# Twelve raw chunks gathered into the tiles of layer 0's weights and of the row vectors

## Chip, core and metric

One core of one Trainium2 chip. The metric is the device time of one launch in microseconds (us); the time of a kernel is the median of its runs. One further execution was recorded by the hardware profiler, and all rows quoted below are of that one. The engines are PE (matmuls), DVE (vector), ACT (scalar, activations), POOL (here the engine that issues gathers) and SP (here only the queue that issues plain transfers).

## What is computed

A graph with N = 6250 nodes of D = 512 features and E = 100000 edges, sorted by destination. Cut to what matters:

```
h = relu(layernorm(x))                         # no weights
norm[e] = -dinv[src[e]] * dinv[dst[e]]         # dinv = 1/sqrt(number of edges that leave a node), 0 for none
prop(h)[n] = sum over edges e into n of h[src[e]] * norm[e]
layer 1: h = leaky(layernorm(h @ W1_0 + prop(h) @ W1_1 + b1) * gamma + beta)   # slope 0.01
layer 2: out = h @ W2_0 + prop(h) @ W2_1 + b2
return x + out
```

All in fp32. The program calls the layers 0 and 1.

## The kernel before

**Stages.** A first stage loads x in 49 blocks of 128 rows, takes each block's mean and variance, makes relu(layernorm(x)), writes it into a table in HBM (`tab[0]`), and counts the edges that leave each node with one-hot matrices on DVE (L341) and matmuls. Then the two layers run one after the other, layer 0 reading `tab[0]` and writing `tab[1]`, layer 1 reading `tab[1]` and writing the output.

**Chunks and gathers.** The edges are cut into 782 chunks of 128. For each chunk POOL issues one indirect DMA that gathers 128 rows of a table, one for each edge, into a slot of the tile `places` (L237 in the first stage, L448 in the layers, L458 for the first 24 of layer 1). A row of `tab[0]` has 528 columns: 512 features, and behind them the node's dinv, so that DVE can scale the chunk's selection matrix by it (`scale`, L614).

**Raw chunks.** The first RAW = 64 chunks of layer 0 do not wait for the table. They are gathered from x itself as soon as the edges' sources are known, and made into relu(layernorm(x)) * dinv in place later: `find` (L481, matmuls that spread a chunk's indices, and a comparison on DVE) and `look_up` (L496, matmuls that fetch each edge's scale and bias; three DVE operations; then four activations, L507). One call of each does four chunks. They run three times a group of layer 0, until all raw chunks are done.

**Slots.** `places` has 63 slots. In the first stage the slots from 14 on hold the blocks of x; the 14 before them are free at once. Each block frees its slot when its write to the table has landed, and then a raw chunk may be gathered there (`make_table`, L306 to 315). The last eight slots later hold layer 1's weights (`w_late`), so the ring of gathers has R = 55 slots: chunk t goes to slot t modulo 55 and must wait until chunk t - 55 has been summed.

**Groups.** Three chunks make a unit, which covers 32 consecutive nodes; four units make a group (66 groups, g from 0; group g holds chunks 12g - 9 to 12g + 2). For a group DVE makes a 0/1 matrix (`choose`, L575), PE multiplies it with the gathered rows (`sums`, L627, 24 matmul passes), and ACT copies the result out (L637). When all groups that touch a block of 128 nodes are there, the block has its turn: `place` puts the groups' sums in the block's rows (L657), `first_half` transposes them and multiplies the block's own rows with W1_0 (`w_sb[1]`), `second` multiplies the sums with W1_1 (`w_sb[0]`), both at L536, and `finish` adds the bias and takes the layernorm (L718 to 740, with `bias1`, `gam`, `bet`).

**Order.** PE, POOL and SP run in the order in which the program is written; ACT and DVE are ordered by the scheduler. POOL's order is all gathers, one after the other. SP's order is in the first stage: loads of x, writes to the table, W1_1 after the first table write, four rows of 2 KB for the vectors, W1_0, the rest of the table, the dinv column of the first 31 blocks (L394); then loads of a block's own rows h two turns ahead (L513), and the blocks' results.

**Vectors.** `b1`, `b2`, `gamma` and `beta` are loaded as one row each (L205). After group 1 `widen` (L847 to 852) spreads each over 128 partitions by a matmul with a column of ones and a copy on DVE.

Of the kernel before, what the change touches and what calls it, by code (L numbers as in the profile page):

```python
# [9 lines left out]
F32 = mybir.dt.float32  # L10
# [3 lines left out]
OP = mybir.AluOpType  # L14
# [6 lines left out]
P = 128  # L21
# [4 lines left out]
Q = 32  # L26
NQ = P // Q
STEP = 3
DRIFT = 32
RE = 14  # L30
RAW = 64
PAD = 16
LATE = 3
AHEAD_OF = 24
# [9 lines left out]
def gnn_kernel(  # L44
# [33 lines left out]
    nc = tc.nc  # L78
    N, D = x.shape
# [5 lines left out]
    KD = D // P  # L85
    NC = -(-E // P)
# [4 lines left out]
    unit = [max(0, NU - NQ * (NS - g)) for g in range(NS + 1)]  # L91
# [16 lines left out]
    ident = const.tile([P, P], F32, name="ident")  # L108
# [13 lines left out]
    bias1 = const.tile([P, D], F32, name="bias1")  # L122
    bias2 = const.tile([P, D], F32, name="bias2")
    gam = const.tile([P, D], F32, name="gam")
    bet = const.tile([P, D], F32, name="bet")
    sidx = const.tile([P, NC], I32, name="sidx")
    eidx = const.tile([P, AHEAD_OF], I32, name="eidx")
    e_src = const.tile([P, AHEAD_OF, LATE], F32, name="e_src")
    w_sb = [const.tile([P, KD, D], F32, name=f"w{i}") for i in range(2)]
    sc = const.tile([P, 2, NB], F32, name="sc")  # L130
    pick = const.tile([P, P], BF, name="pick")
    src_lo = const.tile([P, P], BF, name="src_lo")
    src_hi = const.tile([P, RAW], F32, name="src_hi")
    p_id = const.tile([P, 1], F32, name="p_id")
# [4 lines left out]
    places = stay.enter_context(tc.tile_pool(name="places", bufs=1)).tile([P, RE + NB, W], F32, name="places")  # L139
    w_at = NB - 2 * KD  # L140
    R = RE + w_at
    w_late = places[:, R:, :D].rearrange("p (i k) d -> p i k d", i=2)

    nodes_ps = stay.enter_context(tc.tile_pool(name="nodes_ps", bufs=1, space=bass.MemoryType.PSUM)).tile(
        [P, D], F32, name="nodes_ps")
    assert NQ * NS + 1 <= D - P
# [15 lines left out]
    for ids, fill, name in ((src, 0, "src_c"), (dst, NO_NODE, "dst_c")):  # L162
        t = ep.tile([P, NG, P], I32, name=name)
# [17 lines left out]
    def load_x(i0, n):  # L181
        t = places[:, RE + i0 : RE + i0 + n, :D]
        full = sum(r == P for r in rows[i0 : i0 + n])
        if full:
            nc.sync.dma_start(t[:, :full, :],
                              x[i0 * P : (i0 + full) * P, :].rearrange("(i p) d -> p i d", p=P))
        for lo, hi in parts(rows[i0 + n - 1]) if full < n else ():
            at = (i0 + full) * P
            nc.sync.dma_start(t[lo:hi, full, :], x[at + lo : at + hi, :])
# [5 lines left out]
    def load_rest(k):  # L195
        if k < 3:
            load_x(*groups[6 + k])
        if k == 2:
            nc.sync.dma_start(tab[1][zero_row : zero_row + 1, :], places[P - 1 : P, RE + NB - 1, :D])
        if k == 3:  # L200
            for t, w in zip(w_sb, (W1_1, W1_0)):
                nc.sync.dma_start(t, w.rearrange("(k p) d -> p k d", p=P))
        if k == 1:
            for t, v in ((bias1, b1), (bias2, b2), (gam, gamma), (bet, beta)):
                nc.sync.dma_start(t[0:1], dup(v, 1))  # L205

    LO = P // 2
    HI = 2 * NB
# [15 lines left out]
    with tc.tile_pool(name="turn", bufs=1) as wp, tc.tile_pool(  # L224
        name="turn_ps", bufs=2, space=bass.MemoryType.PSUM
# [7 lines left out]
            nc.scalar.activation(sidx[:, g * P : g * P + n], fT[:, :n], AF.Copy)  # L233

    def gather_raw(lo, hi):
        for t in range(lo, min(hi, R)):
            nc.gpsimd.indirect_dma_start(  # L237
                out=places[:, t, :D], out_offset=None, in_=x,
                in_offset=bass.IndirectOffsetOnAxis(ap=sidx[:, t : t + 1], axis=0))

    gather_raw(0, RE)

    low = ep.tile([P, P], I32, name="low")
    nc.vector.tensor_single_scalar(low, chunks[0][:, 0, :], P - 1, op=OP.bitwise_and)
# [6 lines left out]
    with tc.tile_pool(name="turn", bufs=1) as wp, tc.tile_pool(  # L251
        name="turn_ps", bufs=1, space=bass.MemoryType.PSUM
# [23 lines left out]
        nc.vector.tensor_scalar_mul(minus, last, -1.0)  # L276
        high = ep.tile([P, RAW], I32, name="high")
        nc.vector.tensor_single_scalar(high, sidx[:, :RAW], 7, op=OP.arith_shift_right)
        nc.vector.tensor_copy(src_hi, high)
# [26 lines left out]
    def make_table(i0, n):  # L306

        for lo in range(i0, i0 + n, 2):
            hi = min(lo + 2, i0 + n)
            for i in range(lo, hi):  # L310
                v = places[:, RE + i, :D]
                nc.scalar.activation(v, v, AF.Relu, bias=nb_all[:, i : i + 1], scale=rs_all[:, i : i + 1])
            nc.sync.dma_start(tab[0][lo * P : hi * P, :].rearrange("(i p) d -> p i d", p=P),
                              places[:, RE + lo : RE + hi, :])
            gather_raw(RE + lo, RE + hi)

    some = [*groups[:6], (groups[6][0], NB - LAST - groups[6][0])]
    others = [(NB - LAST, groups[7][0] - (NB - LAST)), *groups[7:]]
# [6 lines left out]
    with tc.tile_pool(name="deg", bufs=1) as dp, tc.tile_pool(name="onehot", bufs=2) as ohp, tc.tile_pool(  # L325
        name="deg_ps", bufs=1, space=bass.MemoryType.PSUM
# [10 lines left out]
        for g in range(EJ // (2 * GJ)):  # L337
            hot = []
            for s, n, name in ((s_lo, LO, "lo"), (s_hi, HI, "hi")):
                t = ohp.tile([EP, GJ, n, 2], BF, name=name)  # L340
# [5 lines left out]
            k = turns.get(g)  # L346
# [15 lines left out]
    with tc.tile_pool(name="fold", bufs=1) as dp, tc.tile_pool(  # L362
        name="fold_ps", bufs=1, space=bass.MemoryType.PSUM
# [3 lines left out]
        for t in range(2):  # L367
            for i in range(2):
                nc.tensor.matmul(deg[t * LO : (t + 1) * LO, :], each[:, i, :], both[:, :, t, i],
                                 start=(i == 0), stop=(i == 1))  # L370
# [38 lines left out]
def usual_path(tc, have):  # L409
    nc = tc.nc  # L410
    (x, out, tab, h_tab, ndinv, sidx, dlx, iota_r, w_sb, W2_1, W2_0, w_late, ident, eps, ones, first, nodes_ps, node_of, minus,
     unsorted, dinv, sdinv, bias1, bias2, gam, bet, unseen, unit, N, E, D, NB, NC, NU, NS, KD, rows, places, R,
     load_rest, sc, pick, src_lo, src_hi, eidx, e_src, zero_row, p_id) = (
        have[n] for n in ("x out tab h_tab ndinv sidx dlx iota_r w_sb W2_1 W2_0 w_late ident eps ones first nodes_ps node_of "
                          "minus unsorted dinv sdinv bias1 bias2 gam bet unseen unit N E D NB NC NU NS KD rows places "
                          "R load_rest sc pick src_lo src_hi eidx e_src zero_row p_id").split())
    AHEAD = 2
    EARLY = {NB - 3: NS - 11, NB - 2: NS - 9, NB - 1: NS - 7}
    ACT = mybir.EngineType.Activation
# [8 lines left out]
    with ExitStack() as es:  # L428
        pool = es.enter_context(tc.tile_pool(name="main", bufs=2))
        psum = es.enter_context(tc.tile_pool(name="main_ps", bufs=2, space=bass.MemoryType.PSUM))  # L430
        es.enter_context(tc.manual_schedule(engines={PE, POOL, SP}))
        is_lo, found, looked, gathered = [], 0, 0, R
        behind, behind_rows, summed = {}, {}, {}
        own_h, own_x, agg, placed, started, pre, late, theres = {}, {}, {}, {}, {}, {}, {}, {}
        SHIFTED = D - D % P
# [3 lines left out]
        own_row, begun = {}, set()  # L439

        def zr(layer, t):
            return places[:, (layer * NC + t) % R, :D]

        def gather_to(layer, end):
            nonlocal gathered
            for t in range(gathered, min(end, NC)):
                own_scale = layer == 0 and t >= RAW
                nc.gpsimd.indirect_dma_start(  # L448
                    out=places[:, t % R, :] if own_scale else zr(layer, t), out_offset=None,
                    in_=x if layer == 0 and t < RAW else tab[layer],  # L450
                    in_offset=bass.IndirectOffsetOnAxis(
                        ap=lidx[:, t - SHIFTED : t - SHIFTED + 1] if layer and t >= SHIFTED else sidx[:, t : t + 1], axis=0))
            gathered = max(gathered, min(end, NC))
# [21 lines left out]
        def find(tag):  # L475
            nonlocal found
            if found == RAW:
                return
# [124 lines left out]
        def scale(sel, chunk, of=(0, NQ)):  # L603

            at = chunk[0][0]
            start = chunk[of[0]][0]
            end = chunk[min(of[1], len(chunk)) - 1][-1] + 1
            if end <= RAW:
                return
            each = sel.rearrange("p q s e -> p (q s) e")  # L610
            cut = sorted({start, end} | {t for t in range(start, end) if t % R == 0})
            for lo, hi in zip(cut, cut[1:]):
                v = each[:, lo - at : hi - at, :]
                last = nc.vector.tensor_tensor(  # L614
                    v, v, places[:, lo % R : lo % R + hi - lo, D : D + 1].to_broadcast([P, hi - lo, Q]), op=OP.mult)
            return last

        def sums(layer, g, sel, chunk, cnt=None, some=None, opens=True, closes=True):
# [65 lines left out]
        def end_block(layer):  # L684

            r = rows[END]
            aT = pool.tile([P, KD, P], F32, name="hT", bufs=1)
            nc.vector.tensor_copy(aT[:, :, :r], placed.pop(END)[:, :, :r])
            return aT
# [147 lines left out]

        find("ps")
        find("ps")
        load_rest(3)  # L840
        for i in range(AHEAD):
            load(0, i)
        for k in range(2):
            look_up("u_ps")
            find("ps")

        def widen():  # L847

            for t in (bias1, gam, bet, bias2):
                ps = psum.tile([P, D], F32, name="u_ps")  # L850
                nc.tensor.matmul(ps, ident[0:1, 0:1].to_broadcast([1, P]), t[0:1, :], start=True, stop=True)
                nc.vector.tensor_copy(t, ps)

        for layer in range(2):
            if layer == 1:
                gathered = AHEAD_OF
# [3 lines left out]
            for g in range(NS - 1):  # L860
# [44 lines left out]
                if layer == 0 and g == 13:  # L905
                    end_matrices()
                if layer == 0 and g == 1:
                    widen()
                if layer == 0 and g == NS - 16:
                    with tc.issue_after(scaled.ins):  # L910
                        shift(0, SHIFTED)
# [21 lines left out]
                if g == NS - 2:  # L933
# [30 lines left out]
                    end = end_block(layer)  # L964
# [333 lines left out]
```

## Time and profile before

| | |
|---|---|
| median of 3 runs | 2038.8 us (2034.94 to 2040.26) |
| profiled execution | 2041.34 us, its span 2039.4 us |
| mean granted clock of PE | 0.911 |
| busy: PE, POOL, DVE, ACT | 82%, 74%, 34%, 20% |
| moved by DMA | 527 MB, 259 GB/s over the span |
| first gather from the table | 132.83 us |
| layer 0 ends, first gather of layer 1 that needs all of its rows | 1066.69 us |
| last gather | 2016.58 us |

The profile's page gives busy times by engine, the span in 40 slices, the DMA queues, the chain of waits that ended last, and the costliest groups of instructions. A row of the timeline reads: start in us, duration in us, engine, line, operation, what it writes and reads, shape, count, and in brackets the engine's idle time before it with what ended it. A row of the view of windows reads: window, length, busy time of PE, PEld (weight loads), DVE, ACT and POOL with the number of their instructions, then the granted PE clock, the DMA share and GB/s. L numbers are lines of the kernel before.

### The profile page before, as it was taken

Reading aid. Unit: us, or ns where it says so; the run is one execution under the profiler, and the core shown is the slowest. Engines: PE = TensorE matmul, PEld = TensorE weight load, DVE = VectorE, ACT = ScalarE, POOL = GpSimd, SP = SyncE. Lnnn points to the kernel's source line nnn. Section 1 sums busy time; section 2 is a strip of 40 time slices with the busy share of each in tenths; the row PEclk is TensorE's granted clock in tenths of the full one; section 3 lists DMA queues with packets and bytes.
Section 4 is the critical chain, followed back from the end, with each engine's and each line's share of the span. In section 5 each row is a group of like instructions: output and inputs, shape, how many; then the busy total and the mean of one; then the engine's idle time right before and its main releaser. Section 6 shows DMA issues by size and latency. Waiting matters only on the chain.

```text
span 2039.4 us, 19969 instructions
## 1 busy us (share of the span) xinstructions
PE 1675.8 (82%) x6864; PEld 669.4 (33%) x6864; DVE 702.2 (34%) x1484; ACT 404.8 (20%) x738; POOL 1517.1 (74%) x1578
## 2 busy tenths in 40 slices
PE   5589987678797767887889888889888887988997
PEld 4454432223333222333333322223332332332333
DVE  7975543333453333443452221122121212121221
ACT  8784211111221111221210101001010010010110
POOL 5877777777777777777777777777777777777774
PEclk9789998889988888988999988899998899999999
DMA  9998888888888888888887888788788888888875
GB/s 350 377 310 256 274 263 253 255 240 263 282 277 253 253 258 246 262 268 252 247 258 238 247 251 251 240 257 252 240 256 248 247 249 256 247 246 251 274 237 161
DMA packets 189546, 527.46 MB, mean 259 GB/s; under 512 B 34576, under 2 KB 36350, under 8 KB 189436
## 3 DMA queue, kind: packets, MB, share of 16 engines
q0 software_dynamic: 125120, 415.98, 68.2%
q1 hardware_dynamic: 64316, 110.12, 15.1%
q8 instruction: 56, 0.92, 0.2%
q14 instruction: 54, 0.44, 0.1%
HBM read 474.31 MB, written 51.66 MB: 258 GB/s over the span
## 4 chain that ended last, share of the span: by engine, by line
PE 45%; DMA 23%; POOL 13%; issue 11%; DVE 6%; ACT 1%; DVEq 0%; POOLq 0%; ACTq 0%; SPq 0%
PE u_ps L536 18%; DMA places<-tab,sidx 16%; PE ps L627 14%; POOL places L448 13%; PE an_ps L657 8%; DMA places<-tab,lidx 6%; PE hT_ps L761 2%; PE hT_ps L524 2%; DVE hi L341 1%; DVE lo L341 1%; PE hT_ps L496 1%; DVE sel L614 1%; DVE st L721 0%; DMA places<-in_x_dram 0%; DVE u_ps L718 0%
## 5 line engine op out<-in xcount | busy, mean ns | idle before, releaser
L448 POOL DMA_INDIRECT places<-tab,sidx x1206 | 1147.3, 951 | 370.8 <-issue 272.2
L627 PE MATMUL ps<-places,sel 128*32 128x512 f32 x3128 | 521.2, 683 | 154.9 <-DMA places<-tab,sidx 84.1
L657 PE MATMUL an_ps<-agg,there 128*128 128x512 f32 (+1 forms) x572 | 279.8, 623 | 103.5 <-ACT agg L637 98.8
L448 POOL DMA_INDIRECT places<-tab,lidx x270 | 255.7, 947 | 82.3 <-issue 63.4
L627 PEld LDWEIGHTS ps<-places,sel 128*32 128x32 f32 x3128 | 104.5, 119 | 542.5 <-issue 200.8
L575 DVE TENSOR_TENSOR sel<-dlx,nodes_ps 128x384 f32<-128x384 f32 (+3 forms) x134 | 72.2, 540 | 416.4 <-PE ps L627 416.3
L536 PE MATMUL u_ps<-w,hT 128*128 128x512 f32 (+1 forms) x400 | 182.3, 599 | 14.8 <-ACT hT L526 14.1
L637 ACT ACTIVATE agg<-ps 128x512 f32<-128x512 f32 (+1 forms) x132 | 78.3, 593 | 569.9 <-PE ps L627 547.1
L536 PE MATMUL u_ps<-places,hT 128*128 128x512 f32 (+2 forms) x408 | 183.4, 593 | 2.2 <-ACT hT L526 2.2
L657 PEld LDWEIGHTS an_ps<-agg,there 128*128 128x128 f32 (+1 forms) x572 | 108.9, 199 | 228.1 <-ACT agg L637 115.6
L536 PE MATMUL u_ps<-w,aT 128*128 128x512 f32 x384 | 174.6, 598 | 1.8 <-DVE aT L763 1.8
L536 PE MATMUL u_ps<-places,aT 128*128 128x512 f32 x384 | 173.3, 593 | 0.8 <-DVE aT L763 0.8
L614 DVE TENSOR_TENSOR sel<-sel,places 128x384 f32<-128x384 f32 (+11 forms) x73 | 35.3, 486 | 377.8 <-DMA places<-tab,sidx 369.1
L712 DVE TENSOR_TENSOR u_ps<-u_ps,bias 128x512 f32<-128x512 f32 x46 | 32.2, 700 | 289.1 <-PE u_ps L536 289.1
L526 ACT ACTIVATE hT<-hT_ps 128x512 f32<-128x512 f32 (+1 forms) x98 | 58.2, 594 | 281.7 <-PE hT_ps L524 281.3
L645 DVE TENSOR_SCALAR there<-iota_r,node_of 128x128 f32<-128x128 f32 (+1 forms) x286 | 85.9, 303 | 60.0 <-PE an_ps L657 57.3
L724 ACT ACTIVATE sd<-mv,eps 128x1 f32<-128x1 f32 (+1 forms) x49 | 14.4, 294 | 463.4 <-DVE mv L722 463.4
L237 POOL DMA_INDIRECT places<-in_x_dram,sidx x55 | 79.0, 1437 | 36.6 <-issue 8.8
L754 ACT ACTIVATE an<-an_ps,ndinv 128x512 f32<-128x512 f32 x96 | 65.8, 685 | 203.4 <-PE an_ps L657 203.3
L536 PEld LDWEIGHTS u_ps<-w,hT 128*128 128x128 f32 (+1 forms) x400 | 72.6, 192 | 88.8 <-issue 73.2
L536 PEld LDWEIGHTS u_ps<-places,hT 128*128 128x128 f32 (+1 forms) x408 | 74.7, 193 | 76.5 <-issue 72.3
L536 PEld LDWEIGHTS u_ps<-w,aT 128*128 128x128 f32 x384 | 71.5, 192 | 82.1 <-issue 78.1
(175 smaller groups left out, 1268.8 us busy)
## 6 DMA issues: line engine op xcount, KB each, us to landing
places<-tab,sidx POOLq DMA_INDIRECT x1206, 3.8
h_tab<-g SPq DMA_DIRECT2D x48, 256.0 KB
xt<-in_x_dram SPq DMA_DIRECT2D x48, 256.0 KB
out_dram<-t SPq DMA_DIRECT2D x48, 256.0 KB
h<-tab SPq DMA_DIRECT2D x46, 256.0 KB
tab<-t SPq DMA_DIRECT2D x46, 256.0 KB
h<-h_tab SPq DMA_DIRECT2D x46, 256.0 KB
tab<-places SPq DMA_DIRECT2D x22, 528.0 KB
```

Of the source, the lines that this page charges most:

```text
L237: nc.gpsimd.indirect_dma_start(out=places[:, t, :D], out_offset=None, in_=x, in_offset=bass.IndirectOffsetOnAxis(ap=sidx[:, t : t + 1], ax ...
L341: nc.vector.tensor_tensor(t, s[:, g * 2 * GJ : (g + 1) * 2 * GJ].rearrange("p (j s) -> p j s", s=2)[:, :, None, :] .to_broadcast([EP, GJ, ...
L448: nc.gpsimd.indirect_dma_start(out=places[:, t % R, :] if own_scale else zr(layer, t), out_offset=None, in_=x if layer == 0 and t < RAW el ...
L526: nc.scalar.activation(hT[:, :, :r], ps[:, :, :r], AF.Copy)
L536: nc.tensor.matmul(u_ps[:r], hT[:, kc, :r], w[:, kc, :], start=(start and kc == 0), stop=(stop and kc == KD - 1))
L575: nc.vector.tensor_tensor(sel[:, q : q + k, :w, :], of, node[:, q : q + k, None, :].to_broadcast([P, k, w, Q]), op=OP.is_equal)
L614: last = nc.vector.tensor_tensor(v, v, places[:, lo % R : lo % R + hi - lo, D : D + 1].to_broadcast([P, hi - lo, Q]), op=OP.mult)
L627: nc.tensor.matmul(ps[q * Q : (q + 1) * Q, :], sel[:, q, s, :], zr(layer, chunk[q][s]), start=(s == 0), stop=(s == len(chunk[q]) - 1 and ( ...
L637: nc.scalar.activation(agg[g][: n * Q], ps[: n * Q], AF.Copy)
L645: behind[1] = nc.vector.tensor_scalar(t[:m, :r], iota_r[:m, :r], node_of[:m, g : g + 1], -(1.0 + i * P), op0=OP.subtract, op1=OP.is_equal)
L657: nc.tensor.matmul(placed[i][:r], t[:m, :r], agg[g][:m, :], start=(g == inside[i][0]), stop=(g == inside[i][-1]))
L754: nc.scalar.activation(an[:r], placed.pop(i)[:r], AF.Copy, scale=ndinv[:r, i : i + 1])
```

## The change

The tiles of layer 0's two weights (eight rows of 128 x 512) and of the four vectors are 12 places of a slot's size. The change lends them to the first X = 12 chunks (`lent`). So 26 chunks and not 14 are gathered before a block of x has to be out of the way, and RAW grows from 64 to 76: chunks 0 to 11 lie in the lent tiles, 12 to 66 in the 55 slots, 67 to 75 follow in the ring, which now counts from chunk 12. The distance in the ring stays 55.

The weights are loaded when chunks 0 to 11 have been summed: `load_rest(3)` stands after the sums of group 1, where `widen` stood. On SP these transfers come behind the first two loads of h and ahead of the third. With them come the vectors, each now as a transfer of 128 x 512 that reads the same row 128 times; `widen` is gone. `find` and `look_up` run 19 times, not 16; the three added calls fall around group 5. Lines before and after differ by 3 or 4 (L237 is L239, L448 is L451, L536 is L539, L627 is L631).

```diff
-RAW = 64
+RAW = 76
...
+    lent = [t[:, k, :] for t in w_sb for k in range(KD)] + [bias1, bias2, gam, bet]
+    X = len(lent)
...
         if k == 3:
             for t, w in zip(w_sb, (W1_1, W1_0)):
                 nc.sync.dma_start(t, w.rearrange("(k p) d -> p k d", p=P))
-        if k == 1:
             for t, v in ((bias1, b1), (bias2, b2), (gam, gamma), (bet, beta)):
-                nc.sync.dma_start(t[0:1], dup(v, 1))
+                nc.sync.dma_start(t, dup(v, P))
...
     def gather_raw(lo, hi):
-        for t in range(lo, min(hi, R)):
+        for t in range(lo, min(hi, X + R)):
             nc.gpsimd.indirect_dma_start(
-                out=places[:, t, :D], out_offset=None, in_=x,
+                out=lent[t] if t < X else places[:, t - X, :D], out_offset=None, in_=x,
                 in_offset=bass.IndirectOffsetOnAxis(ap=sidx[:, t : t + 1], axis=0))
 
-    gather_raw(0, RE)
+    gather_raw(0, X + RE)
...
-            gather_raw(RE + lo, RE + hi)
+            gather_raw(X + RE + lo, X + RE + hi)
...
         def zr(layer, t):
-            return places[:, (layer * NC + t) % R, :D]
+            k = layer * NC + t
+            return lent[k] if k < X else places[:, (k - X) % R, :D]
...
-        load_rest(3)
         for i in range(AHEAD):
             load(0, i)
...
-        def widen():
-
-            for t in (bias1, gam, bet, bias2):
-                ps = psum.tile([P, D], F32, name="u_ps")
-                nc.tensor.matmul(ps, ident[0:1, 0:1].to_broadcast([1, P]), t[0:1, :], start=True, stop=True)
-                nc.vector.tensor_copy(t, ps)
...
                 if layer == 0 and g == 1:
-                    widen()
+                    assert STEP * unit[g + 1] >= X
+                    load_rest(3)
```

More of the change, by code (lines that the diff above doesn't have):

```diff
@@ L412, in usual_path @@
      unsorted, dinv, sdinv, bias1, bias2, gam, bet, unseen, unit, N, E, D, NB, NC, NU, NS, KD, rows, places, R,
-     load_rest, sc, pick, src_lo, src_hi, eidx, e_src, zero_row, p_id) = (
+     load_rest, sc, pick, src_lo, src_hi, eidx, e_src, zero_row, p_id, lent, X) = (
         have[n] for n in ("x out tab h_tab ndinv sidx dlx iota_r w_sb W2_1 W2_0 w_late ident eps ones first nodes_ps node_of "
                           "minus unsorted dinv sdinv bias1 bias2 gam bet unseen unit N E D NB NC NU NS KD rows places "
-                          "R load_rest sc pick src_lo src_hi eidx e_src zero_row p_id").split())
+                          "R load_rest sc pick src_lo src_hi eidx e_src zero_row p_id lent X").split())
     AHEAD = 2
@@ L431, in usual_path @@
         es.enter_context(tc.manual_schedule(engines={PE, POOL, SP}))
-        is_lo, found, looked, gathered = [], 0, 0, R
+        is_lo, found, looked, gathered = [], 0, 0, X + R
         behind, behind_rows, summed = {}, {}, {}
@@ L448, in gather_to @@
                 nc.gpsimd.indirect_dma_start(
-                    out=places[:, t % R, :] if own_scale else zr(layer, t), out_offset=None,
+                    out=places[:, (t - X) % R, :] if own_scale else zr(layer, t), out_offset=None,
                     in_=x if layer == 0 and t < RAW else tab[layer],
@@ L610, in scale @@
             each = sel.rearrange("p q s e -> p (q s) e")
-            cut = sorted({start, end} | {t for t in range(start, end) if t % R == 0})
+            cut = sorted({start, end} | {t for t in range(start, end) if (t - X) % R == 0})
             for lo, hi in zip(cut, cut[1:]):
                 v = each[:, lo - at : hi - at, :]
+                k = (lo - X) % R
                 last = nc.vector.tensor_tensor(
-                    v, v, places[:, lo % R : lo % R + hi - lo, D : D + 1].to_broadcast([P, hi - lo, Q]), op=OP.mult)
+                    v, v, places[:, k : k + hi - lo, D : D + 1].to_broadcast([P, hi - lo, Q]), op=OP.mult)
             return last
```

## The prediction

> **What bounds the kernel now.** I read the page first: the busy line, the slices, the chain, the costliest groups.
>
> ```profile
> span 2039.4 us, 19969 instructions
> PE 1675.8 (82%) x6864; PEld 669.4 (33%) x6864; DVE 702.2 (34%) x1484; ACT 404.8 (20%) x738; POOL 1517.1 (74%) x1578
> POOL 5877777777777777777777777777777777777774
> PE 45%; DMA 23%; POOL 13%; issue 11%; DVE 6%; ACT 1%; DVEq 0%; POOLq 0%; ACTq 0%; SPq 0%
> L448 POOL DMA_INDIRECT places<-tab,sidx x1206 | 1147.3, 951 | 370.8 <-issue 272.2
> ```
>
> PE is busiest and has most of the chain, but POOL's digit is an even 7 to the end. A gather takes 951 ns, and the idle time before it is split into equal bits, so 7 tenths may be all that POOL can do. The view of waits, asked for POOL over the whole span, decides that:
>
> ```profile
> POOL places L448 <- issue: 336.5, 1104, 0.3
> POOL places L448 <- DMA tab<-pre: 2.2, 1, 2.2
> ```
>
> No wait of the 1104 is over 0.3 us: it is the step between two gathers, not a wait for anybody. Under other names too that view has nothing over 0.3 for L448, but for this 2.2 and the 1.64 shown next. POOL's timeline gives the rest (gathers counted in order: 29.69 is chunk 13, 40.00 chunk 14, 50.67 chunk 16, 83.39 chunk 28, 90.19 chunk 31, 132.83 chunk 64, 170.37 chunk 94, 185.39 chunk 106, 2016.58 the last of all):
>
> ```profile
> 29.69 2.53 POOL L237 DMA_INDIRECT places<-in_x_dram,sidx  x1 [0.30 <-issue]
> 40.00 1.93 POOL L237 DMA_INDIRECT places<-in_x_dram,sidx  x1 [7.78 <-ACT junk L292]
> 50.67 1.66 POOL L237 DMA_INDIRECT places<-in_x_dram,sidx  x1 [6.96 <-ACT junk L296]
> 83.39 1.95 POOL L237 DMA_INDIRECT places<-in_x_dram,sidx  x1 [2.21 <-ACT places L312]
> 90.19 0.95 POOL L237 DMA_INDIRECT places<-in_x_dram,sidx  x1 [0.30 <-DMA tab<-places]
> 132.83 0.94 POOL L448 DMA_INDIRECT places<-tab,sidx  x1 [1.64 <-ACT places L507]
> 170.37 0.94 POOL L448 DMA_INDIRECT places<-tab,sidx  x1 [0.30 <-issue]
> 185.39 0.95 POOL L448 DMA_INDIRECT places<-tab,sidx  x1 [0.30 <-issue]
> 2016.58 0.95 POOL L448 DMA_INDIRECT places<-tab,lidx  x1 [0.30 <-issue]
> ```
>
> From 132.83 to 170.37 stand 30 gathers: 1.251 us each. From 132.83 on POOL stops once, for 2.2 us at the turn of the layers. So the end is the start of the table gathers, plus 1.251 us for each that is left, plus a tail of 22.8 us (2039.4 - 2016.58). Whatever lets POOL have more gathers behind it early moves the end by as much, unless something stops POOL later. POOL's stops lie in the first stage: 7.78, 6.96, 2.21 and 1.64 us, 18.6 us in all.
>
> **The change, part by part.** *Twelve more gathers that wait for nothing.* 26 chunks, not 14, can be gathered before a block of x must be written to the table. Until DVE's one-hots end at 89 us a gather is slow:
>
> ```profile
> L237 POOL DMA_INDIRECT places<-in_x_dram,sidx x27 | 52.4, 1940 | 24.3 <-ACT junk L292 8.1 <-ACT junk L296 7.6 <-issue 5.5
> ```
>
> 1.940 + 0.30 = 2.24 us each (window 14 to 89.5 us). After chunk 13 ends (32.2 us), 57 us of this stretch hold 25.4 gathers, now without the stops: 39.4 behind it, against 30.5. The other 36.6 of the 76 raw ones take 45.8 us: the first table gather is at 135.3 us, as chunk 76. Before, chunk 76 came at 132.83 + 12 x 1.251 = 147.8. POOL's own lead is 12.5 us. Bounds: at 2.83 us each (the row at 29.69 and its step) 5.9 us; and 15.0 us, since the table is not there before 132.83. I take 12.5, from the mean of 27.
>
> *The bytes.* DMA is full in this stage:
>
> ```profile
> 33.00:60.00 27.00, 17.49 (x144) 15.47 (x144) 26.98 (x23) 26.17 (x66) 12.12 (x5) 0.81 1.03 380
> 90.00:120.00 30.00, 14.53 (x105) 11.19 (x105) 26.08 (x81) 25.67 (x39) 22.71 (x24) 0.72 1.02 377
> ```
>
> (The last two columns are DMA share and GB/s.) 12 gathers of 262 KB come in, 3.15 MB; two weights of 1.05 MB go out. 1.05 MB at 0.377 MB/us is 2.8 us at most, and with 9 gathers of lead at 120 us only 0.6. The table lands at 133.4 to 135.6, when POOL comes. ACT and DVE, 26 of 27 us busy there, hide later x loads. I take nothing here.
>
> *The ring holds POOL back.* There are still 55 slots: chunk t needs chunk t - 55 summed. Here PE's timeline counts; the sums (L627) at 119.79, 166.09 and 177.18 are groups 1, 4 and 5.
>
> ```profile
> 119.79 3.12 PE L627 MATMUL ps<-places,sel 128*32 128x512 f32 x24
> 122.84 1.12 PE L851 MATMUL u_ps<-bias,ident 1*128 1x512 f32 x2
> 127.27 1.21 PE L496 MATMUL hT_ps<-sc,xt 128*128 128x98 f32 x8
> 139.97 0.39 PE L481 MATMUL hT_ps<-src_lo,pick 128*128 128x128 bf16 x4
> 153.39 3.60 PE L536 MATMUL u_ps<-w,hT 128*128 128x512 f32 x8
> 159.99 3.60 PE L536 MATMUL u_ps<-w,aT 128*128 128x512 f32 x8
> 166.09 2.78 PE L627 MATMUL ps<-places,sel 128*32 128x512 f32 x24
> 168.81 1.13 PE L496 MATMUL hT_ps<-sc,xt 128*128 128x98 f32 x8
> 177.18 2.78 PE L627 MATMUL ps<-places,sel 128*32 128x512 f32 x24
> 160.00:265.00 105.00, 105.00 (x466) 42.91 (x465) 52.80 (x118) 32.56 (x56) 79.40 (x85) 1.00 0.87 269
> ```
>
> Chunk 39 is the first of group 4, free at 166.09 + 2 x 2.78/24 = 166.3. Chunk 94 takes its slot at 170.37. So POOL has 4.0 us of room here, and of a lead of 12.5 it keeps only 4.0 plus what PE gains before group 4.
>
> *What PE gains and pays.* The spreading of the vectors (L851) goes: 127.27 - 122.84 = 4.4 us, not hidden, since PE is the late one here. One more pick of indices falls before group 4: 0.39 us and its hand-over, 0.5. And the weights, loaded late, may make PE wait: next.
>
> *The weights' arrival.* SP issues them behind the two first loads of h, these behind the dinv column of the table:
>
> ```profile
> 111.86 0.96 SPq L394 DMA_DIRECT2D tab<-dinv  x1
> q1 hardware_dynamic: 4213, 0.44, 36.0%
> q1 hardware_dynamic: 288, 0.52, 19.7%
> 549.09 2.00 SPq L864 DMA_DIRECT2D places<-in_L_gnn_W_dram  x2
> q1 hardware_dynamic: 1279, 2.50, 42.1%
> q1 hardware_dynamic: 1316, 2.56, 36.4%
> DMA packets 2529, 6.68 MB, mean 352 GB/s; under 512 B 307, under 2 KB 307, under 8 KB 2527
> ```
>
> The q1 rows (packets, MB) are the DMA view in windows 120 to 133, 132 to 139, 549 to 565 and 549 to 568; the last row is all queues of the last window. The column's 4213 packets hold SP's queue until about 132.5; the two loads of h follow (0.52 MB). Group 1's sums, which the weights wait for, end at 122.9: no hindrance. So 2.62 MB must pass. The late weights of layer 1 are the same two transfers beside the same gathers: 2.50 MB in 16 us, or 2.56 MB in 19. At these rates W1_0 has landed at 149.3 or 151.9. PE needs it for the products at 153.39, now at 149.0: a wait of 0.3 to 2.9 us. I take 1.0, nearer the first, as the last 3 us of the wider window moved only 0.06 MB.
>
> By the Trainium skill ("DMA: Bandwidth & Descriptors", Queues, rings and completion order) an engine takes turns between the queues that have work, a packet at a time. Half of the 352 GB/s of that window would land W1_0 at 147.4, the wait would be nothing and the gain 7.9 us. The trace speaks against an even split: 156 GB/s and less for q1.
>
> *The rest.* Vectors: 1.05 MB more, landed by 156 to 160; the first add needs them after the products at 159.99, 163.6 - 4.4 + 1.0 = 160.2: nothing, or up to 1 us of DVE. Queued on SP behind the weights' wait are the vectors and h of blocks 2 and 3, and h of block 2 is used in the third turn only; behind POOL's waiting gather stand only later gathers. Three look-ups are added around group 5: 1.13 us and a hand-over of 0.45 each, two of them with picks before group 5, so 3.9 us of PE. Group 5 starts 4.4 - 1.0 - 0.5 - 3.9 = 1.0 us later, and chunk 106 (185.39, slot free at 177.4 before) keeps a lead of 7.0. ACT's 12 more scalings lie in a stretch where it is busy 32.56 of 105 us, and DVE, with 52.80, hides its share. Twelve fewer chunks are multiplied by their own scale and two index operations are 12 columns wider: nothing, beside that idle time of DVE.
>
> **Sum:** lead kept 4.0 + 4.4 - 0.5 - 1.0 = 6.9 us. That the rest of layer 0 follows, PE full to 265, is seen here:
>
> ```profile
> DVE sel L614 <- DMA places<-tab,sidx: 369.1, 50, 14.6
> ```
>
> DVE waits 369 us for gathered rows in layer 0, so PE is pulled by POOL again and the end of the layer moves along. The profiled execution took 2041.34 us (span 2039.4, 1.9 around it): 2034.4. The median shown is 2038.8, 2.5 lower: 2031.9, or -0.34%.
>
> **Rivals.** *A, slower: the weights come late.* Place: the first products with W1_0. Each us of wait is one of lead lost; from 7.9 us of wait (landing after 156.9) the kernel is slower. The lowest rate in the trace for this queue beside gathers is 0.52 MB in 7 us: 2.62 MB would take 35 us, landing at 167.9, wait 18.9, 11 us slower: 2049.8. Against it: in that window only 0.52 MB were asked for. For it: a wait also costs clock, as here:
>
> ```profile
> 272.59 2.08 PE L657 MATMUL an_ps<-agg,there 128*128 128x512 f32 x2 [5.25 <-ACT agg L637]
> 271.70:278.30 6.60, 5.71 (x22) 1.49 (x26) 4.71 (x12) 3.13 (x6) 4.80 (x6) 0.50 0.84 245
> ```
>
> After a stop of 5.25 us PE had half its clock for 6.6 us: 3.3 us more, and the point falls to 153.6. The Trainium skill ("TensorE: Matmul & The Clock Gate", What's actually happening) says this comes from about 3.4 us of idleness; by that rule a wait of 4 us would cost 7, the trace agrees (0.50), and a wait of 1 us nothing.
>
> *B, more: the ring does not hold.* PE's half clock before 138 us may fall elsewhere, and the weights come in time: the lead is POOL's own, 12.5: 2026.3. Against it: room of 4.0.
>
> *C, no change: the lead is lost again or never made*: by 2 to 5 us of wait, by POOL reaching only the bound of 5.9, or at the turn of the layers, where POOL already waits 2.2 us for the last table rows: if PE's end does not move, all 6.9 are given back, 2038.8. Against it: the 369 us.
>
> **Chances** (0.3%, or 6.1 us, is about what a measurement of this kernel can tell from no change). Forecast, lead 6.1 to 9: 0.36. B: 0.16. C, gain under 6.1: 0.22. A: 0.26, clock included, of which 0.07 under 6.1 us and 0.19 over. Faster 0.52, same 0.29, slower 0.19. The range holds B at 2026 and A as far as 2046; its last 4 us to the bound are left out.
>
> **What would show it.** POOL: no stops of 7 us before 90, first table gather (chunk 76) at 135 +- 4, then stops of 1 to 5 us on PE's sums before chunk 94, which is issued near 163.5, and none later but at the turn. PE: no spreading rows, a wait of about 1 us before the first products at 149 to 150. The last gather at 2009.7. I am wrong if W1_0's products start after 157, if POOL stops after chunk 106, or if the wait at the turn grows from 2.2 us by as much as the lead.

## The result, and the profile after

The changed kernel takes 2031.54 us (median of 21 runs, 2026.64 to 2037.71), the kernel before 2037.66 us (21 runs, 2032.90 to 2042.12): a ratio of 0.997, 95% interval 0.9962 to 0.9978, so 6.1 us or 0.3% less. The profiled execution took 2031.3 us with a span of 2029.5; that of the kernel before took 2041.34, 3.7 us over its own median. Some experiments ran on two chips on which the kernel before itself takes 2450 to 2474 us; their times are compared only with its times there, and stand in a part of their own.

The page of the changed kernel, the lines that answer to those shown of before:

```profile
span 2029.5 us, 20041 instructions
PE 1664.2 (82%) x6892; PEld 667.0 (33%) x6892; DVE 704.8 (35%) x1490; ACT 413.2 (20%) x750; POOL 1520.1 (75%) x1578
POOL 7876777777777777777777777777777777777774
PE 47%; DMA 23%; POOL 12%; issue 10%; DVE 5%; ACT 1%; DVEq 0%; POOLq 0%; ACTq 0%; SPq 0%
L451 POOL DMA_INDIRECT places<-tab,sidx x1194 | 1133.5, 949 | 372.0 <-issue 260.7
```

Two of POOL's digits show the change: the first, 7 instead of 5, since POOL no longer stops in the first 50 us, and the fourth, 6 instead of 7, since it stops later, between 152 and 203 us. The rest is seen in POOL's timeline (gathers counted in order: 35.40 is chunk 15, 129.37 chunk 70, 131.25 chunk 71, 137.50 chunk 76, 167.07 chunk 94, 182.08 chunk 106, 2009.90 the last), and in the view of waits, asked for POOL (total, times, longest):

```profile
35.40 2.53 POOL L239 DMA_INDIRECT places<-in_x_dram,sidx  x1 [0.30 <-issue]
129.37 1.10 POOL L451 DMA_INDIRECT places<-in_x_dram,sidx  x1 [1.75 <-PE ps L631]
131.25 0.94 POOL L451 DMA_INDIRECT places<-in_x_dram,sidx  x1 [0.78 <-ACT places L510]
137.50 0.95 POOL L451 DMA_INDIRECT places<-tab,sidx  x1 [0.30 <-issue]
167.07 0.94 POOL L451 DMA_INDIRECT places<-tab,sidx  x1 [7.36 <-PE ps L631]
182.08 0.95 POOL L451 DMA_INDIRECT places<-tab,sidx  x1 [0.30 <-PE ps L631]
2009.90 0.95 POOL L451 DMA_INDIRECT places<-tab,lidx  x1 [0.30 <-issue]
```

```profile
POOL places L451 <- PE ps L631: 32.6, 79, 7.4
POOL places L451 <- DMA tab<-pre: 1.6, 1, 1.6
```

The stops of 7.78, 6.96 and 2.21 us before 90 are gone. Chunk 76 leaves 10.3 us earlier than before (137.50 against 147.84). Then one stop of 7.36 us, on PE's sums of group 4, takes 7 of these 10.3: chunk 94 leaves 3.3 us earlier (167.07 against 170.37), and chunk 106 too (182.08 against 185.39). The last gather leaves 6.7 us earlier (2009.90 against 2016.58), and the tail behind it is 19.6 us (2029.5 - 2009.90), not 22.8. Of the 9.9 us between the two spans, then, the change's lead at chunk 94 is only 3.3. The rest came elsewhere: 0.6 at the turn of the layers (a stop of 1.6, not 2.2), 2.8 from a gather that is 2 ns shorter (949 against 951, over 1470 of them), 3.2 in the tail. The last two seem to come with the execution: the five kernels profiled below on chips of this speed have 949 or 950 ns, four of them tails of 19.5 to 20.2 us and one 21.4, and two of the four gain nothing. Since the kernel before has only one profile on such a chip, this is not shown.

PE's timeline between groups 3 and 4 (sums L631 at 141.46 and 165.28, the first products L539 at 148.59) shows what held group 4 up:

```profile
141.46 2.78 PE L631 MATMUL ps<-places,sel 128*32 128x512 f32 x24
146.60 0.38 PE L484 MATMUL hT_ps<-src_lo,pick 128*128 128x128 bf16 x4 [1.30 <-ACT hT L529]
148.59 6.70 PE L539 MATMUL u_ps<-w,hT 128*128 128x512 f32 x8 [0.77 <-DMA w<-in_L_gnn_W_dram]
155.13 1.03 PE L499 MATMUL hT_ps<-sc,xt 128*128 128x98 f32 x8
159.18 3.60 PE L539 MATMUL u_ps<-w,aT 128*128 128x512 f32 x8
165.28 2.78 PE L631 MATMUL ps<-places,sel 128*32 128x512 f32 x24
```

Group 3 is 6.9 us earlier than before (141.46 against 148.33), group 4 only 0.8 (165.28 against 166.09). Between them lie a stop of 1.30 us for ACT, one of 0.77 us for W1_0, and products of 6.70 us instead of 3.60. Busy time by windows (PE, PEld, DVE, ACT, POOL, then the granted clock, DMA share, GB/s) explains two of them; first before, then after:

```profile
130.00:140.00 10.00, 9.77 (x55) 5.47 (x55) 5.20 (x12) 9.25 (x13) 6.60 (x7) 0.58 0.96 308
140.00:150.00 10.00, 8.29 (x56) 4.48 (x57) 7.01 (x16) 8.11 (x12) 7.56 (x9) 1.00 0.82 242
```

```profile
130.00:140.00 10.00, 8.28 (x61) 5.03 (x54) 8.18 (x19) 10.00 (x16) 7.08 (x8) 1.00 0.98 345
144.40:147.80 3.40, 1.91 (x16) 1.38 (x15) 2.18 (x5) 3.19 (x6) 2.49 (x4) 1.00 1.04 384
147.80:151.20 3.40, 2.63 (x4) 1.18 (x4) 1.35 (x3) 2.93 (x4) 2.54 (x3) 0.51 1.03 357
151.20:154.60 3.40, 3.40 (x5) 1.35 (x4) 0.00 (x0) 0.00 (x1) 2.73 (x3) 0.50 1.05 396
```

ACT, 9.25 of 10 us busy from 130 to 140 before, is now busy for all 10: the scalings of the raw chunks (L510) keep it until the copy of hT that PE waits for. And after a stretch of 3.4 us with PE busy for 1.91, its clock was halved for 6.8 us, just when the products ran. Finer windows show when it fell:

```profile
147.60:147.80 0.20, 0.20 (x3) 0.00 (x0) 0.20 (x2) 0.00 (x0) 0.20 (x1) 1.00 0.80 302
147.80:148.00 0.20, 0.03 (x1) 0.00 (x0) 0.20 (x1) 0.00 (x0) 0.20 (x1) 0.59 0.92 350
```

A mean of 0.59 means that the clock fell at about 147.84. PE's wait for W1_0 runs from 147.82 to 148.59, so it had only begun: the stretch ahead of the fall holds the stop of 1.30 us for ACT and not this wait.

### The profile page after: what moved, and what is told of

It reads as the page before. It is cut to its first block, busy times and chain, and to the rows that moved or that the text cites. A ratio compares the mean times of both kernels' runs of the same rounds, so it can differ in the third digit from the quotient of the medians.

```text
span 2029.5 us, 20041 instructions
## 1 busy us (share of the span) xinstructions
PE 1664.2 (82%) x6892; PEld 667.0 (33%) x6892; DVE 704.8 (35%) x1490; ACT 413.2 (20%) x750; POOL 1520.1 (75%) x1578
## 4 chain that ended last, share of the span: by engine, by line
PE 47%; DMA 23%; POOL 12%; issue 10%; DVE 5%; ACT 1%; DVEq 0%; POOLq 0%; ACTq 0%; SPq 0%
PE u_ps L539 19%; DMA places<-tab,sidx 17%; PE ps L631 14%; POOL places L451 12%; PE an_ps L661 9%; DMA places<-tab,lidx 5%; PE hT_ps L765 2%; PE hT_ps L527 2%; DVE hi L343 1%; DVE lo L343 1%; DMA w<-in_L_gnn_W_dram 1%; PE both_ps L357 1%; DVE sel L618 0%; ACT places L510 0%; PE hT_ps L499 0%
## 5 line engine op out<-in xcount | busy, mean ns | idle before, releaser
L451 POOL DMA_INDIRECT places<-tab,sidx x1194 | 1133.5, 949 | 372.0 <-issue 260.7
L631 PE MATMUL ps<-places,sel 128*32 128x512 f32 x3104 | 507.6, 663 | 146.9 <-DMA places<-tab,sidx 86.3
L451 POOL DMA_INDIRECT places<-tab,lidx x270 | 255.2, 945 | 82.2 <-issue 58.8
L631 PEld LDWEIGHTS ps<-places,sel 128*32 128x32 f32 x3104 | 102.0, 117 | 526.7 <-issue 189.8
L539 PE MATMUL u_ps<-w,hT 128*128 128x512 f32 (+1 forms) x400 | 185.3, 607 | 15.2 <-ACT hT L529 13.7
L539 PE MATMUL u_ps<-places,hT 128*128 128x512 f32 (+2 forms) x408 | 183.7, 594 | 2.2 <-ACT hT L529 2.2
L539 PE MATMUL u_ps<-w,aT 128*128 128x512 f32 x384 | 174.8, 598 | 2.2 <-DVE aT L767 2.2
L539 PE MATMUL u_ps<-places,aT 128*128 128x512 f32 x384 | 173.3, 593 | 0.8 <-DVE aT L767 0.8
L539 PEld LDWEIGHTS u_ps<-w,hT 128*128 128x128 f32 (+1 forms) x400 | 73.6, 194 | 91.0 <-issue 74.7
L539 PEld LDWEIGHTS u_ps<-places,hT 128*128 128x128 f32 (+1 forms) x408 | 74.8, 193 | 76.7 <-issue 72.5
L539 PEld LDWEIGHTS u_ps<-w,aT 128*128 128x128 f32 x384 | 71.2, 192 | 82.8 <-issue 78.0
L539 PEld LDWEIGHTS u_ps<-places,aT 128*128 128x128 f32 x384 | 70.7, 190 | 79.9 <-issue 78.8
```

The lines of the kernel that those rows point to most:

```text
L451: nc.gpsimd.indirect_dma_start(out=places[:, (t - X) % R, :] if own_scale else zr(layer, t), out_offset=None, in_=x if layer == 0 and t < ...
L539: nc.tensor.matmul(u_ps[:r], hT[:, kc, :r], w[:, kc, :], start=(start and kc == 0), stop=(stop and kc == KD - 1))
L631: nc.tensor.matmul(ps[q * Q : (q + 1) * Q, :], sel[:, q, s, :], zr(layer, chunk[q][s]), start=(s == 0), stop=(s == len(chunk[q]) - 1 and ( ...
```

## Experiments

**The gain by its parts.** Four kernels on one chip, beside 24 runs of the kernel before there (median 2035.26 us).

*no_lend* takes the lending out and leaves the late loads:

```diff
-    X = len(lent)
+    X = 0
...
-RAW = 76
+RAW = 64
```

> One part alone: the weights and vectors are loaded late and the vectors are spread by their DMA as in the changed kernel, but no chunk is gathered into their tiles; 64 raw chunks and 14 free gathers as before. Theory (the gain is POOL's lead from the twelve free gathers): first table gather at 133 us as before, time 2037.7, as before, give or take 1. Rival (the gain comes from the 4.4 us of PE that the spreading took, or from 2 MB less of early loads): 2033 to 2035.

Measured: 2034.02 us (11 runs), ratio 0.9997 (0.9988 to 1.0005). POOL's timeline; 131.74 is the first table gather (chunk 64), 169.26 chunk 94:

```profile
131.74 0.94 POOL L451 DMA_INDIRECT places<-tab,sidx  x1 [3.04 <-ACT places L510]
169.26 0.95 POOL L451 DMA_INDIRECT places<-tab,sidx  x1 [0.30 <-ACT places L510]
```

POOL is where it was before (132.83 and 170.37, 1.1 us apart), with no stop over 0.8 us on PE's sums. The expectation's times were set against 2037.7 us for the kernel before; here that kernel takes 2035.26, so the 2034.02 in the rival's range decides nothing, and the ratio counts: a gain of 0.6 us, between 2.4 us of gain and 1.0 of loss. Late weights and spread vectors alone bring nothing that can be told from no change: the gain needs the twelve chunks. The rival falls.

*ring63* leaves the change and takes the ring's hold away: the eight places that later take layer 1's weights serve the first lap as slots.

```diff
+    S = 2 * KD
+    def slot(k):
+        j = k - X
+        return j if j < R + S else (j - S) % R
...
-            return lent[k] if k < X else places[:, (k - X) % R, :D]
+            return lent[k] if k < X else places[:, slot(k), :D]
...
-                gather_to(layer, STEP * unit[g] + R)
+                at = STEP * unit[g] + R
+                gather_to(layer, at if layer else max(at, min(at + S, X + S + 2 * R)))
```

> The changed kernel with eight more slots for the first lap of the ring: the eight places that later hold the weights of layer 1, so that a chunk of the first lap needs the chunk 63 before it summed, not the one 55 before. Theory (the ring takes 7 of POOL's 10.3 us of lead at chunk 94): no stop on PE's sums before chunk 94, which is issued at about 160 us, lead 10.3 us against before, and the kernel takes 7.0 us less than the changed one: 2024.5. Rival (something else stops POOL at the same place, rows of the table or PE itself): chunk 94 stays near 167 and the time at 2031.5. A lead lost again later, at the turn of the layers or at the ring's second lap, would show as a chunk 94 near 160 with a time of 2028 to 2031.

Measured: 2024.35 us (6 runs), ratio 0.9951 (0.9938 to 0.9963). POOL's timeline (135.44 is chunk 76, 157.95 chunk 94, 2001.93 the last gather) and its waits for the sums:

```profile
135.44 0.95 POOL L456 DMA_INDIRECT places<-tab,sidx  x1 [0.30 <-issue]
157.95 0.95 POOL L456 DMA_INDIRECT places<-tab,sidx  x1 [0.31 <-issue]
2001.93 0.95 POOL L456 DMA_INDIRECT places<-tab,lidx  x1 [0.30 <-issue]
```

```profile
POOL places L456 <- PE ps L636: 19.2, 63, 0.3
```

The stop is gone (longest wait 0.3 us), chunk 94 leaves 9.1 us earlier than in the changed kernel, and the last gather 8.0. So the ring did hold POOL, and nothing else stood behind it. The time fell by 10.0 us against before (0.0049 x 2035.26) where the change gives 6.1: 3.9 more, not the 7.0 expected, though the medians themselves, which were not measured side by side, lie 7.2 apart. This is the fastest version tried.

*w_first* loads W1_0 ahead of W1_1:

```diff
-            for t, w in zip(w_sb, (W1_1, W1_0)):
+            for t, w in zip(w_sb[::-1], (W1_0, W1_1)):
```

> The changed kernel with the two weights of layer 0 loaded in the other order: W1_0, which the first products read, ahead of W1_1. Theory (the lead that POOL keeps is set by when PE sums group 4, and PE loses 0.77 us to W1_0 and 3.1 us to half the clock in the first products, 6.70 instead of 3.60): W1_0 lands some 6 us earlier, the first products start at about 147.8 us and take 3.6, group 4's sums move from 165.3 to 161.4, chunk 94 from 167.1 to about 163.2, and the kernel takes 3.9 us less than the changed one: 2027.6. Rival 1 (the half clock comes from the short stops before these products, not from W1_0): only the wait goes, 0.8 us, 2030.7. Rival 2 (what PE does here sets nothing): 2031.5.

Measured: 2028.83 us (6 runs), ratio 0.9965 (0.9953 to 0.9977). PE's timeline (first products, sums of group 4), POOL's (chunk 94), and the window at the products:

```profile
148.68 0.66 PE L765 MATMUL hT_ps<-ident,an 128*128 128x128 f32 x4 [0.19 <-ACT an L758]
149.17 3.60 PE L539 MATMUL u_ps<-w,hT 128*128 128x512 f32 x8
162.75 2.78 PE L631 MATMUL ps<-places,sel 128*32 128x512 f32 x24
```

```profile
164.54 0.94 POOL L451 DMA_INDIRECT places<-tab,sidx  x1 [3.38 <-PE ps L631]
```

```profile
147.80:151.20 3.40, 2.91 (x13) 1.65 (x13) 2.12 (x4) 2.72 (x5) 2.78 (x3) 1.00 1.04 403
```

The wait for W1_0 and the half clock are gone, and from the first products to group 4 it is 13.6 us instead of 16.7. But the order of the weights is not shown to be the reason. *ring63* has the changed kernel's order and the same stop for ACT, and yet no wait for W1_0 and no half clock:

```profile
148.42 0.38 PE L489 MATMUL hT_ps<-src_lo,pick 128*128 128x128 bf16 x4 [1.30 <-ACT hT L534]
149.49 3.60 PE L544 MATMUL u_ps<-w,hT 128*128 128x512 f32 x8
```

From these products to its group 4 (163.07) it is 13.6 us too, and *no_lend*, again with that order, starts its products at 147.94 with no wait and at full clock. So the theory, that the 3.1 us of half clock come from the wait for W1_0, fails: the clock fell when the wait had only begun. Rival 1 names the stops that do lie ahead of the fall, but they are still there in *w_first* and halve nothing; when they do is open (see the last section). Chunk 94 came 2.5 us earlier. The time is 1.0 us lower by the ratios, inside both intervals: a gain from the order is not shown.

*widen_back* puts work as long as the old spreading back into the changed kernel, with results that nobody reads:

```diff
                     load_rest(3)
+                    for k in range(4):
+                        ps = psum.tile([P, D], F32, name="u_ps")
+                        nc.tensor.matmul(ps, ident[0:1, 0:1].to_broadcast([1, P]), dlx[0:1, :D], start=True, stop=True)
+                        nc.vector.tensor_copy(pool.tile([P, D], F32, name="t"), ps)
```

> The changed kernel with the four spreading products and their four copies put back at their old place behind group 1's sums, as work whose result nobody reads (one row of the edges' targets is spread into a scratch tile). Theory (PE's time up to group 4 is POOL's lead): 4.4 us more of PE, of which 2.3 us may lie in the stops that PE has at 145 to 148.6 us; chunk 94 2.1 to 4.4 us later than 167.1, time 2033.6 to 2035.9. Rival 1 (with these stops filled the half clock of the first products goes too, 3.1 us): chunk 94 within 1.3 us of 167.1, time 2030.5 to 2032.8. Rival 2 (PE's time here is hidden): chunk 94 unchanged, 2031.5.

Measured: 2035.51 us (11 runs), ratio 0.9997 (0.9988 to 1.0006). PE's timeline behind group 1's sums, and POOL's at chunks 70 and 94:

```profile
126.12 3.78 PE L908 MATMUL u_ps<-dlx,ident 1*128 1x512 f32 x4 [0.22 <-DVE t L909]
129.83 2.03 PE L499 MATMUL hT_ps<-sc,xt 128*128 128x98 f32 x8
137.59 3.84 PE L631 MATMUL ps<-places,sel 128*32 128x512 f32 x24
```

```profile
139.77 0.98 POOL L451 DMA_INDIRECT places<-in_x_dram,sidx  x1 [10.16 <-PE ps L631]
171.14 0.94 POOL L451 DMA_INDIRECT places<-tab,sidx  x1 [1.23 <-PE ps L631]
```

Four small products and their copies take back the whole gain, 5.5 us by the ratios, more than the 4.4 that they took in the kernel before: as there, PE falls to half its clock behind them (a look-up takes 2.03 us, not 1.13), and group 2's sums begin 9.5 us later than in the changed kernel (137.59 against 128.05; 1.4 of it was there at group 1's sums). The half clock at this place stands in both profiles with the spreading, and in none of the five without it. POOL now stops 10 us at chunk 70 already. Both rivals fall; dropping the spreading was as necessary as the lending.

Over these four, chunk 94 and the time move together. Against *no_lend* (169.26 and 2034.02): *w_first* -4.7 and -5.2 us, *ring63* -11.3 and -9.7, *widen_back* +1.9 and +1.5. These times are medians; by the time of the profiled execution itself it is -2.9, -8.0 and +4.2 us, so order and sign hold, but the sizes agree only within 3.3 us.

**Fewer chunks lent.** *vectors_lent*, on another chip (before there: 2035.17 us, 15 runs), lends the four vectors' tiles only and loads the weights early as before:

```diff
-    lent = [t[:, k, :] for t in w_sb for k in range(KD)] + [bias1, bias2, gam, bet]
+    lent = [bias1, bias2, gam, bet]
...
-RAW = 76
+RAW = 68
```

> One part alone: only the four vectors' tiles are lent (4 chunks, 68 raw ones); the weights are loaded at their old early place, the vectors spread by their DMA after group 1's sums. Theory (POOL's own lead is at most what is lent, 4 x 1.251 = 5.0 us, which the ring hardly cuts, and no wait for weights comes with it): first table gather, chunk 68, at 132 to 134 us, no stop over 1 us between it and chunk 94, which comes at 164 to 166, and the time 4 to 6 us under that of the kernel before, nearly as good as with twelve. Rival (the gain goes by the number of chunks lent): a third of the changed kernel's 6.1 us, 2 us.

Measured: 2031.61 us (11 runs), ratio 0.9985 (0.9976 to 0.9994): 3.1 us less than before, between theory and rival, so it decides neither. POOL's timeline: chunk 59, the first into a slot already summed, chunk 68, the first from the table, and chunk 94:

```profile
125.71 1.15 POOL L452 DMA_INDIRECT places<-in_x_dram,sidx  x1 [4.04 <-ACT places L511]
137.16 0.95 POOL L452 DMA_INDIRECT places<-tab,sidx  x1 [0.30 <-issue]
170.20 0.94 POOL L452 DMA_INDIRECT places<-tab,sidx  x1 [0.30 <-issue]
```

In this execution POOL stopped 4.04 us at chunk 59, the table gathers began 3 us later than the theory said, and chunk 94 has no lead at all (170.20 against 170.37); it took 2033.95 us, 2.3 over its median. Half of the changed kernel's gain is there with a third of the chunks; by which way, this profile does not show.

**The chips of 2450 us.** Here I sought the price of late weights, *weights_twice* loading both weights twice at the late place, and second profiles of both kernels.

```diff
-            for t, w in zip(w_sb, (W1_1, W1_0)):
+            for t, w in zip(w_sb * 2, (W1_0, W1_1, W1_1, W1_0)):
```

> The changed kernel with both weights of layer 0 loaded twice at the late place, so that W1_0 lands with the last of 4.2 MB: rival A's price doubled. Between 129 and 152 us the queue moved 3.75 MB, 0.163 MB a us, so 2.1 MB more take 12.9 us. Theory (each us by which the weights are late is one of lead lost): the first products start near 161.5 instead of 148.6, group 4's sums come at 178 to 180, chunk 94 at 180 to 182, 10 to 12 us later than in the kernel before, and the time is 8 to 13 us above that of the kernel before. Rival (the lead comes back later, or other work of PE fills the wait): under 5 us above the kernel before.

> The kernel before once more, for a second profile. The first one's last gather left at 2016.6 us with a tail of 22.8 us, while the changed kernel's stood at 2009.9 with a tail of 19.6, though the lead at chunk 94 is only 3.3 us. If the tail and the wider step between gathers (1.2520 against 1.2510 us) belong to the execution and not to the kernel, this profile has a tail nearer 20 us or a step of 1.2510; if they belong to the kernel, both come back.

> The changed kernel once more, for a second profile and its time beside the others on one chip. Theory: chunk 94 is issued 3 to 7 us earlier than in the kernel before's second profile, held by PE's sums of group 4, and the time is 5 to 7 us under that of the kernel before. If the half clock of the first products is chance, it may be absent here, and chunk 94 then comes near 164.

Measured: *weights_twice* 2453.83 us against 2451.63, ratio 1.0001 (0.9973 to 1.0029); the same kernel twice on the other of the two chips, *w_twice* 1.0024 (1.0001 to 1.0047) and *w_doubled* 1.0042 (1.0009 to 1.0074). *after_again* 2483.09 against 2473.90, ratio 1.0039 (1.0012 to 1.0066): not 5 to 7 us less, as expected, but 9.6 more. *before_again* 2474.22. The kernel of *vectors_lent*, as *vec_only* 1.0004 (0.9985 to 1.0023) and as *vec_lent* 0.9978 (0.9952 to 1.0005). The profile of *before_again*, the chain that ended last and POOL's waits:

```profile
PE 30%; another core or an unknown queue 22%; issue 21%; POOL 13%; DVE 7%; DMA 5%; ACT 2%; POOLq 0%; DVEq 0%; SPq 0%; ACTq 0%
```

```profile
POOL places L448 <- remote: 243.8, 99, 4.8
POOL places L448 <- PE ps L627: 120.4, 36, 14.0
POOL places L448 <- DMA tab<-pre: 19.9, 1, 19.9
```

A fifth of the chain is waits for something outside the records, and POOL stops for PE's sums all through the kernel, 120 us in all, where in the first profile it had no such stop over 0.3 us. So the end hangs on more than POOL's own rate there, and a lead of POOL at chunk 94 need not reach it; why the changed kernel is even slower is not shown. Neither theory on the weights is tested by this. What a weight 13 us late costs stays open. The gather of 954 ns and the tail of 60 us (2472.3 - 2411.93) in *before_again* belong to these chips and say nothing of the first profile's.

## Why the prediction was right

It gave 2031.9 us and 6.9 us of gain; 2031.5 and 6.1 were measured. The sign and the mechanism hold: POOL's lead moves the end, as far as the ring lets it through. Several terms of the sum were off, and that the total came so close is in part luck.

- *POOL sets the end:* shown. Over four kernels on one chip the median time followed chunk 94 within 1.6 us, the profiled executions' own times within 3.3.
- *Lead of its own 12.5 us, first table gather at 135.3:* 10.3 and 137.50. The stops before 90 went as predicted; two that I had not looked for came at chunks 70 and 71 (1.75 and 0.78 us), the first on the ring, for group 2's sums. *ring63*, without them, has 135.44.
- *Bytes, nothing:* group 1's sums begin at 119.5, before at 119.79.
- *The ring holds POOL at chunk 94, of 12.5 us only 4.0 and PE's gain pass:* shown; a stop of 7.36 us there, none with 63 slots. Rival B, the ring that does not hold, is what *ring63* makes true: a gain of 10.0 us, where it gave 12.5.
- *PE gains 4.4, pays 0.5:* too small. 6.9 us at group 3, since the half clock that followed the spreading (0.58 from 130 to 140) went with it.
- *W1_0 lands at 149.3 to 151.9, wait 1.0:* it landed at 148.6, ahead of the range, but PE came for it earlier too (147.8, not 149.0), so that the wait of 0.77 is near my 1.0 by luck. The queue moved more than I took from layer 1:

```profile
DMA packets 3449, 8.18 MB, mean 356 GB/s; under 512 B 556, under 2 KB 556, under 8 KB 3448
q0 software_dynamic: 1329, 4.42, 56.4%
q1 hardware_dynamic: 2119, 3.75, 44.3%
```

  These are all queues, POOL's and SP's, from 129 to 152 us (packets, MB): 163 GB/s for SP's queue, 46% of the bytes. That lies between my 156 and the half of 356, 178, and nearer to mine. W1_0's landing lies 1.2 us behind the 147.4 that I had worked out from the turns by packet of the Trainium skill ("DMA: Bandwidth & Descriptors", Queues, rings and completion order), and 0.7 us ahead of my 149.3.
- *A wait of 1 us costs no clock:* not refuted, but a term was missed beside it. A half clock at the first products cost 3.1 us (6.70 against 3.60), four times the wait, and it began before the wait could matter (147.84, the wait from 147.82). Ahead of it lie PE's short stops, 1.30 us for ACT the longest, to which the sum gave no price. In four other profiles with the same stops it did not come, so its size here is partly chance.
- *ACT's added scalings lie in idle time:* they do, from 160 to 265 us, where ACT is now busy 39.42 of 105 us. What I missed lies earlier: from 120 to 146 us ACT is full, and PE, 6.9 us earlier at group 3, has to wait 1.30 us for it. *no_lend*, without the added scalings, has the same stop, so it comes from PE's gain and not from them.
- *A freed slot is used at once:* I took chunk 39's slot free 0.2 us into group 4's sums. Chunk 94 leaves 1.79 us after these begin (165.28 to 167.07; in *w_first* 162.75 to 164.54).
- *Sum:* lead kept 6.9 us, measured 3.3 in the profiled execution. To the predicted 163.5 for chunk 94 come 2.1 us for group 4 (165.28, not 163.2: 3.0 gained at group 3; 3.1 lost to the clock; 1.1 lost ahead of the products, to ACT and the weight; 0.9 in the look-ups behind them, where another pick lies) and 1.5 for the slot: 167.1. The prediction reckoned from a profiled execution that lay 3.7 us above its median, and the changed kernel's lay at its own.
- *The turn gives nothing back:* right, 1.6 instead of 2.2 us.

Why the median gains 6.1 when the profile shows a lead of 3.3 is not settled. The half clock may be a part of it: without its 3.1 us the lead would be 6.4 (an estimate from these rows), and *w_first*, at full clock there, has 5.8 (170.37 - 164.54). How often it comes no run shows. Executions differ in this very place: group 1's sums begin at 119.5 us in the changed kernel's profile and at 121.7 in *w_first*'s, whose program is the same up to there, and both kernels' runs span 9 to 11 us. Rival A, weights late enough to lose, was only seen from its near end: W1_0 came 0.77 us late, and the half clock beside it is not shown to be its price.

## What to carry to other kernels

A lead given to the engine that bounds a kernel is worth what the next limit lets through: here a ring of 55 slots took 7 of 10.3 us, and the place to look is the timeline of whoever frees the slots. Work that is cheap on an engine off the bound counts in full where that engine frees them: four small products undid the gain, since PE's clock fell behind them. When a clock falls beside a wait, look in fine windows which came first: here the wait had only begun, so it can't have been the cause. For effects of a few tenths of a per cent, take several profiles of each kernel, since one chain moves by 2 us from execution to execution.

## What the runs showed of the hardware

PE's clock was halved without PE having stood still. In the changed kernel the 3.4 us from 144.40 had PE busy for 1.91 us, 56%, with no stop over 1.30 us, and the next two such stretches ran at 0.51 and 0.50. In *widen_back* it fell at about 126.1 us although PE had been busy for 3.20 of the 3.40 us before, 94%, the last of them with the products that read one row:

```profile
122.70:126.10 3.40, 3.20 (x17) 0.90 (x9) 3.26 (x10) 3.40 (x6) 2.55 (x3) 1.00 1.13 322
126.10:129.50 3.40, 3.38 (x4) 1.16 (x4) 1.46 (x3) 3.31 (x6) 2.72 (x3) 0.50 1.06 235
```

Nor does a low share of busy time suffice: *no_lend* has the same stops, with PE busy for 1.92 of 3.41 us, and keeps its full clock.

```profile
145.15:148.56 3.41, 1.92 (x14) 1.36 (x14) 2.19 (x6) 2.73 (x6) 2.50 (x4) 1.00 0.99 289
148.56:151.98 3.42, 3.42 (x13) 1.75 (x12) 0.82 (x2) 2.91 (x4) 2.50 (x4) 1.00 1.03 400
```

The Trainium skill ("TensorE: Matmul & The Clock Gate", What's actually happening) speaks of an idle window of about 3.4 us; the trace agrees with the length, half the clock lasting two of them, but not with the idleness. What else decides stays open.
